# Softmax over partitions by GpSimd all-reduces in place of TensorE, and a scheduled TensorE order, in a two-layer graph kernel

## The chip, the cores and the metric

The kernel runs on one core of a Trainium2 chip. Times are device microseconds of one execution. The kernel before took 2955.12 us, the median of three runs (2951.85 to 2955.24).

The engines are called by their names in the profile: PE (TensorE; PEld its weight loads), DVE (VectorE), ACT (ScalarE), POOL (GpSimd) and SP, which here issues all transfers (SPq is its queue).

## The reference

There are 32 batches of a 512 x 512 matrix x and a 512 x 512 matrix adj, all in float32. Two layers follow each other; each normalizes its input, cuts it at zero and adds its result to the input.

```python
# layer 0
h = relu(layernorm(x))
agg = (adj @ h) / max(rowsum(adj), 1e-6)
x = x + relu(concat([h, agg]) @ W.T)           # W: 512 x 1024
# layer 1
h = relu(layernorm(x))
q, k = split(h @ Wqk);  v = h @ Wv
w = inv_scale * mask * sum(q * (adj @ (k * mask)), -1)
x = x + softmax(w, over the 512 rows)[:, None] * v
```

The softmax runs over the 512 rows of a batch: 512 values of w, which lie as 128 partitions x 4 values. Its maximum and its sum must therefore be taken across partitions.

## The kernel before, in words

**Products.** All large products go through `product` (L121), one level of Strassen's method: seven products of 256 x 256 blocks in place of eight, with sums of blocks made beforehand by `left_sums` and `right_sums` (L103, L112) on DVE. Product k is four matmuls with 128 x 256 results (eight for layer 0's output, which has two terms); the profile shows each as two instructions, so that a product stands there as x8. Its results stand in three PSUM tiles, pp, pr and pq; `keep` (L142) copies some of them to SBUF on ACT (m1, u2, m5, u3; the profile writes m_ and u_ with the product's name), and DVE adds them up. After each product `step()` takes one piece of other work from a list, `background`, so that the other engines' instructions are written between the products.

A batch needs five products: y (layer 0's h by the second half of W, `layer0_y`, L289), o (h by the first half plus adj by y, `layer0_out`, L302), u (adj by the masked h of layer 1, `layer1_u`, L345), t (h of layer 1 by a combined matrix of the two halves of Wqk, multiplied by u and summed, `layer1_t`, L356) and v (`layer1_v`, L376).

**Transposes.** The left operand of a product must stand transposed. The kernel writes a matrix to DRAM scratch and reads it back in another order (`exchange`, L171), then DVE turns 32 x 32 blocks (`to_left`, L179, its instruction in L183). This gives hT (layer 0's h), aT (adj) and h1T (layer 1's h). The scratch transfers are dh and sh for hT, da and sa for aT, d and s for h1T.

**Order.** The main loop (L522 on) runs over i = 0 to 32 and overlaps three batches: u of batch i-1, o of batch i, then t and v of batch i-1, then y of batch i+1. Behind t and v lie, through `background`, the normalization of layer 1 of batch i (`layer1_norm`, L317) and the preparation of hT and aT of batch i+1 (`prepare_h`, L230; `prepare_a`, L256). The pieces of the softmax of batch i-1 and of h1T (`layer1_h`, L334) are taken during y. The loop stands under `tc.manual_schedule` for PE: PE's instructions keep the order in which they are written. On the other engines a scheduler orders the instructions, with the written order as priority; each engine then works through its own queue in that order.

**Normalization.** Statistics of a row block are taken by DVE (`statistics`, L208: L210 and L211); `moments` (L213) turns the variance into 1/sqrt by `pow` on POOL (L216), between two small DVE steps (L215 rstd, L217 nmr); ACT normalizes (`normalize`, L221). For layer 0's h (tile n) the result is written to dh; for layer 1's h (tile h1m) it is written to d, and ACT then scales it by the mask (L327).

**Softmax** (`softmax`, L390). s0: DVE adds up w, multiplies it by the degree and the mask, and takes the maximum of its four values per partition (top, L405). s1: PE transposes top into one row of PSUM (ptop, L409), DVE takes the negative maximum (ntop, L410). s2: PE spreads this one value over the partitions by a matmul with a row of ones (pbc, L414), DVE copies it (nbc, L415), ACT takes the exponential (e, L416), DVE sums four values (es, L417). s3: PE sums over partitions by a matmul with a matrix of ones (psum, L421), DVE takes the reciprocal and scales e (rs, L422; sm, L423). s4: DVE adds sm times v to x (L426), and SP writes x out (L433).

Of the kernel before, what the change touches and what calls it, by code (L numbers as in the profile page):

```python
# [11 lines left out]
AF = mybir.ActivationFunctionType  # L12
ALU = mybir.AluOpType
AX = mybir.AxisListType

P = 128
DEG_EPS = 1e-6
# [4 lines left out]
def kernel(  # L22
# [32 lines left out]
    nc = tc.nc  # L55
# [37 lines left out]
    def drain(n=0):  # L93
        while len(background) > n:
            background.pop(0)()
# [87 lines left out]
        nc.vector.transpose(o, t.rearrange("p k (c r) -> p k c r", r=R))  # L183


    ones = const.tile([P, P], F32, name="ones")
    nc.vector.memset(ones, 1.0)
    mhalf = const.tile([P, C], F32, name="mhalf")
    nc.vector.memset(mhalf, -0.5)

# [8 lines left out]
    def load_x(b):  # L199
        X[b] = load_rows("x", 2, x[b], f"x_{b}")  # L200
# [29 lines left out]
    def prepare_h(b):  # L230

        t = norm_tiles(f"0_{b}")
        d = scratch("dh", f"dh_{b}")
        tiles = {}

        def load():
            n = load_rows("n", 2, x[b], f"n_{b}")
            for c in range(C):
                tiles[c] = n[:, c, :]

        def write(c):
            normalize(tiles[c], tiles[c], t, c)
            nc.sync.dma_start(out=d[c], in_=tiles[c])

        def turn(h):
            if h == 0:
                HT[b] = slots("hT", 1, f"hT_{b}")
            to_left(halves(d), h, HT[b], f"sh_{b}_{h}")

        return (  # L250
            [load] + [lambda c=c: statistics(tiles[c], t, c, f"0_{b}") for c in range(C)] + [lambda: moments(t)]
            + [lambda c=c: write(c) for c in range(C)],
            [lambda: turn(0), lambda: turn(1)],
        )
# [47 lines left out]
    def layer0_out(b):  # L302
        def o(r, cc):
            dst = X[b][:, 2 * r:2 * r + 2, ts(cc, H)]

            def f(p, s):
                if s is not None:
                    t = block("tmp", 5, f"o_{b}_{r}{cc}")
                    add(t, p, s)
                    p = t  # L310
                nc.vector.scalar_tensor_tensor(dst, p, 0.0, dst, op0=ALU.max, op1=ALU.add)

            return f

        product(f"o_{b}", [(HT[b], w1R), (AT[b], Y[b])], o(0, 0), o(0, 1), o(1, 0), o(1, 1))

    def layer1_norm(b):  # L317

        mt = norm_tiles(f"1_{b}")
        t = H1M[b] = slots("h1m", 1, f"h1m_{b}")  # L320
        d = H1T[b] = scratch("d1", f"d1_{b}")

        def one(c):
            v = t[:, 2 * (c // 2):2 * (c // 2) + 2, c % 2, :]
            normalize(v, X[b][:, c, :].rearrange("p (a f) -> p a f", a=2), mt, c)
            nc.sync.dma_start(out=d[c].rearrange("p (a f) -> p a f", a=2), in_=v)
            nc.scalar.activation(v, v, AF.Copy, scale=mraw[:, c, b:b + 1])  # L327

        return (
            [lambda c=c: statistics(X[b][:, c, :], mt, c, f"1_{b}") for c in range(C)] + [lambda: moments(mt)]  # L330
            + [lambda c=c: one(c) for c in range(C)] + right_sums(t)
        )
# [12 lines left out]
    def layer1_u(b):  # L345
        u = U[b] = big.tile([P, 4, 2, H], F32, tag="uv", bufs=1, name=f"u_{b}")

        def o(slot):
            return lambda p, s: add(u[:, slot, :, :], p, s)

        product(
            f"u_{b}", [(AT[b], H1M[b])], o(0), o(1),
            lambda p, _: nc.scalar.activation(u[:, 2, :, :], p, AF.Copy), o(3),
        )
# [35 lines left out]
    def softmax(b):  # L390
        acc = W.pop(b)
        w = small.tile([P, C], F32, tag="w", name=f"w_{b}")
        top = small.tile([P, 1], F32, tag="top", name=f"top_{b}")
        ntop = small.tile([1, 1], F32, tag="ntop", name=f"ntop_{b}")
        nbc = small.tile([P, 1], F32, tag="nbc", name=f"nbc_{b}")
        e = small.tile([P, C], F32, tag="e", name=f"e_{b}")
        es = small.tile([P, 1], F32, tag="es", name=f"es_{b}")
        rs = small.tile([P, 1], F32, tag="rs", name=f"rs_{b}")
        sm = small.tile([P, C], F32, tag="sm", name=f"sm_{b}")

        def s0():
            add(w, acc[:, 0, :], acc[:, 1, :])
            nc.vector.tensor_tensor(w, w, DEG[b], op=ALU.mult)
            nc.vector.tensor_tensor(w, w, mcol[:, :, b], op=ALU.mult)
            nc.vector.tensor_reduce(top, w, AX.X, ALU.max)  # L405

        def s1():
            ptop = ps_s.tile([1, P], F32, tag="s", name=f"ptop_{b}")
            nc.tensor.transpose(ptop, top, identity)  # L409
            nc.vector.tensor_reduce(ntop, ptop, AX.X, ALU.max, negate=True)  # L410

        def s2():
            pbc = ps_s.tile([P, 1], F32, tag="s", name=f"pbc_{b}")
            nc.tensor.matmul(pbc, ones[0:1, :], ntop, start=True, stop=True)  # L414
            nc.vector.tensor_copy(nbc, pbc)  # L415
            nc.scalar.activation(e, w, AF.Exp, bias=nbc)  # L416
            nc.vector.tensor_reduce(es, e, AX.X, ALU.add)  # L417

        def s3():
            psum = ps_s.tile([P, 1], F32, tag="s", name=f"psum_{b}")  # L420
            nc.tensor.matmul(psum, ones, es, start=True, stop=True)  # L421
            nc.vector.reciprocal(rs, psum)  # L422
            nc.vector.tensor_scalar(sm, e, rs, None, op0=ALU.mult)  # L423

        def s4(c):
            nc.vector.scalar_tensor_tensor(  # L426
                X[b][:, c, :], V[b][:, c, :], sm[:, c:c + 1], X[b][:, c, :],
                op0=ALU.mult, op1=ALU.add,
            )
            if c == C - 1:  # L430
                t = X.pop(b)
                for q, dst in enumerate(by_rows(out[b])):
                    nc.sync.dma_start(out=dst, in_=t[q * R:(q + 1) * R, :, :])  # L433

        return [s0, s1, s2, s3], [lambda c=c: s4(c) for c in range(C)]


    w1R, w2R, mR, vR = (slots(n, 1, n, const) for n in ("w1R", "w2R", "mR", "vR"))
# [56 lines left out]
    def weights_late():  # L495
        wqT = big.tile([P, C, 512], F32, tag="uv", bufs=1, name="wqT")
        wkT = slots("h1T", 1, "wkT")[:, 0:4, :, :].rearrange("p s b f -> p (s b f)").rearrange("p (c f) -> p c f", c=C)
        weight_rows(wqk[:, 0:F], wqT, True, "wq")
        weight_rows(wqk[:, F:2 * F], wkT, False, "wk")
        for k in range(2):  # L500
            for dk in range(2):
                p = mm_tile(f"pm_{k}{dk}")
                d = 2 * k + dk
                for a in range(C):
                    nc.tensor.matmul(
                        p.rearrange("p a f -> p (a f)"), wqT[:, a, ts(d, P)], wkT[:, a, :],
                        start=(a == 0), stop=(a == C - 1),
                    )
                nc.scalar.activation(mR[:, 2 * k:2 * k + 2, dk, :], p, AF.Copy)
        for s in right_sums(mR):  # L510
            s()
        tv = load_rows("uv", 1, wv, "tv")
        for c in range(C):
            nc.scalar.activation(
                vR[:, 2 * (c // 2):2 * (c // 2) + 2, c % 2, :],
                tv[:, c, :].rearrange("p (a f) -> p a f", a=2), AF.Copy,
            )
        for s in right_sums(vR):
            s()


    with tc.manual_schedule(engines={mybir.EngineType.PE}):  # L522
        for i in range(B + 1):
            norm = prep = []
            if i > 0:
                layer1_u(i - 1)
                drain()
            if i + 1 < B:
                steps, rest = prepare_h(i + 1)
                background += steps  # L530
            if i < B:
                layer0_out(i)
                drain()
                if i == 0:
                    weights_late()
                norm = layer1_norm(i)
            if i + 1 < B:
                prep = rest + [lambda: left_sums(HT[i + 1])[0](), lambda: left_sums(HT[i + 1])[1]()] + prepare_a(i + 1)
            if i > 0:
                background += norm + prep  # L540
                layer1_t(i - 1)
                layer1_v(i - 1)
                drain()
                first, last = softmax(i - 1)
            else:
                for s in norm + prep:
                    s()
                first = last = []
            background += first + last + (layer1_h(i) if i < B else [])
            if i + 1 < B:  # L550
                layer0_y(i + 1)
            drain()
            if i + 1 < B:
                load_x(i + 1)


# [26 lines left out]
```

## Time and profile before

| what | value |
|---|---|
| median of three runs | 2955.12 us |
| the profiled execution, timed | 2955.12 us |
| its span, first to last instruction | 2953.3 us |
| mean granted PE clock | 0.941 |
| PE busy | 2521.0 us (85%) |
| DVE busy | 1465.5 us (50%) |
| ACT busy | 862.6 us (29%) |
| POOL busy, all but 0.7 us of it the 64 `pow` of L216 | 65.2 us (2%) |
| DMA queue of SP, share of 16 engines | 48.4% |
| one iteration of the loop, steady | 90.45 us |

A line of groups names the line of the code, the engine, the operation, output and input tiles, their shapes and the count; then the busy time in us and the mean of one in ns; then the idle time of the engine just before these instructions and what ended most of it. A chain of waits is followed back from the last instruction: at each step to what released it. A timeline gives start, length, engine, line, tiles and, in brackets, the idle time before and what ended it. Ends of matmuls are modelled, so that neighbouring entries overlap a little.

### The profile page before, as it was taken

How to read it: one execution, taken by the hardware profiler on the slowest of the kernel's cores; microseconds unless marked ns; L12 is line 12 of the kernel's file. 1: busy time of each engine (PE TensorE's matmuls, PEld its weight loads, DVE VectorE, ACT ScalarE, POOL GpSimd, SP SyncE). 2: the span in 40 equal slices, each digit the busy share in tenths (PEclk: the TensorE clock that was granted, in tenths of full speed). 3: DMA queues.
4: the chain of work that ended last, by engine and by line, in shares of the span. 5: the costliest groups of instructions: out<-in, count | busy, mean ns of one | idle time of the engine just before them, and what ended most of it. 6: DMA issues, size and time to landing. Idle time of an engine off the chain costs nothing.

```text
span 2953.3 us, 30565 instructions
## 1 busy us (share of the span) xinstructions
PE 2521.0 (85%) x10948; PEld 2145.5 (73%) x10948; DVE 1465.5 (50%) x3105; ACT 862.6 (29%) x1547; POOL 65.2 (2%) x70
## 2 busy tenths in 40 slices
PE   4798988889988889888898888898888988888988
PEld 3577777777777778777787777787777877777876
DVE  4454544544545545445455455454554544544545
ACT  1332223332233322233222333222332223332232
POOL 0000000000000000000000000000000000000000
PEclk8899999999999999999999999999999999999999
DMA  7554456435465344564454553435634545435342
GB/s 152 131 126 113 114 118 143 111 93 130 96 143 131 93 114 103 129 143 106 91 129 104 143 130 87 123 99 133 143 98 98 126 106 143 121 93 125 90 118 57
DMA packets 363784, 342.91 MB, mean 116 GB/s; under 512 B 27216, under 2 KB 264784, under 8 KB 363632
## 3 DMA queue, kind: packets, MB, share of 16 engines
q1 hardware_dynamic: 363632, 340.96, 48.4%
q8 instruction: 86, 1.41, 0.2%
q14 instruction: 66, 0.54, 0.1%
HBM read 206.64 MB, written 134.22 MB: 115 GB/s over the span
## 4 chain that ended last, share of the span: by engine, by line
PE 66%; DVE 12%; ACT 9%; DMA 6%; SPq 4%; issue 2%; POOL 1%; DVEq 0%; POOLq 0%; ACTq 0%
PE pp_o L131 15%; PE pp_y L131 8%; PE pp_u L131 8%; PE pq_o L131 7%; PE pp_t L131 6%; PE pr_o L131 4%; PE pq_u L131 4%; SPq L176 4%; PE pq_t L131 4%; DVE st L210 4%; ACT h1m L221 3%; DMA n<-in_x_dram 3%; ACT a L276 3%; PE pq_y L131 2%; ACT n L221 2%
## 5 line engine op out<-in xcount | busy, mean ns | idle before, releaser
L131 PE MATMUL pp_y<-w2R,hT 128*128 128x256 f32 x1024 | 298.2, 442 | 244.2 <-DVE hT L183 176.0
L131 PEld LDWEIGHTS pp_y<-w2R,hT 128*128 128x128 f32 x1024 | 219.1, 222 | 300.9 <-issue 201.1
L131 PE MATMUL pq_v<-vR,h1T 128*128 128x256 f32 x512 | 171.9, 495 | 132.3 <-ACT m_v L144 132.3
L131 PE MATMUL pp_v<-vR,h1T 128*128 128x256 f32 x1024 | 257.4, 397 | 1.0 <-ACT m_v L144 1.0
L131 PE MATMUL pp_o<-y,aT 128*128 128x256 f32 x1024 | 245.7, 383 | 12.7 <-DVE aT L183 12.7
L131 PEld LDWEIGHTS pq_v<-vR,h1T 128*128 128x128 f32 x512 | 126.3, 253 | 166.8 <-ACT m_v L144 144.0
L131 PE MATMUL pp_u<-h1m,aT 128*128 128x256 f32 x1024 | 243.2, 381 | 0.0
L131 PE MATMUL pp_t<-mR,h1T 128*128 128x256 f32 x1024 | 241.9, 379 | 0.0
L131 PE MATMUL pp_o<-w1R,hT 128*128 128x256 f32 x1024 | 241.9, 379 | 0.0
L131 PEld LDWEIGHTS pp_v<-vR,h1T 128*128 128x128 f32 x1024 | 207.6, 203 | 35.1 <-ACT m_v L144 1.8
L131 PEld LDWEIGHTS pp_o<-y,aT 128*128 128x128 f32 x1024 | 196.6, 192 | 40.3 <-DVE aT L183 13.2
L131 PEld LDWEIGHTS pp_u<-h1m,aT 128*128 128x128 f32 x1024 | 195.2, 191 | 26.7
L131 PEld LDWEIGHTS pp_t<-mR,h1T 128*128 128x128 f32 x1024 | 194.6, 190 | 26.5
L131 PEld LDWEIGHTS pp_o<-w1R,hT 128*128 128x128 f32 x1024 | 194.6, 190 | 26.5
L98 DVE TENSOR_TENSOR o<-m_o,u_o 128x512 f32<-128x512 f32 x32 | 22.1, 692 | 320.6 <-ACT u_o L144 320.6
L131 PE MATMUL pq_y<-w2R,hT 128*128 128x256 f32 x512 | 128.1, 393 | 4.8 <-DVE hT L98 1.5
L101 DVE TENSOR_TENSOR h1m<-h1m 128x512 f32<-128x512 f32 x128 | 85.3, 687 | 90.2 <-ACT h1m L327 89.2
L216 POOL TENSOR_TENSOR rstd<-rstd,mhalf 128x4 f32<-128x4 f32 x64 | 64.5, 1007 | 2822.4 <-DVE rstd L215 2594.4
L144 ACT ACTIVATE u_o<-pp_o 128x512 f32<-128x512 f32 x64 | 38.2, 597 | 294.3 <-PE pp_o L131 294.3
L131 PE MATMUL pq_o<-y,aT 128*128 128x256 f32 x512 | 121.0, 379 | 0.0
L131 PE MATMUL pq_u<-h1m,aT 128*128 128x256 f32 x512 | 121.0, 379 | 0.0
L131 PE MATMUL pq_t<-mR,h1T 128*128 128x256 f32 x512 | 121.0, 379 | 0.0
(121 smaller groups left out, 3702.6 us busy)
## 6 DMA issues: line engine op xcount, KB each, us to landing
n<-in_x_dram SPq DMA_DIRECT2D x128, 256.0 KB, 6.8
dh<-n SPq DMA_DIRECT2D x128, 256.0 KB, 2.0
a<-in_adj_dram SPq DMA_DIRECT2D x128, 256.0 KB, 9.1
sh<-dh SPq DMA_DIRECT2D x256, 128.0 KB, 3.5
x<-in_x_dram SPq DMA_DIRECT2D x128, 256.0 KB, 6.4
da<-a SPq DMA_DIRECT2D x128, 256.0 KB, 2.2
sa<-da SPq DMA_DIRECT2D x256, 128.0 KB, 3.5
d<-h1m SPq DMA_DIRECT2D x128, 256.0 KB, 2.6
```

What stands on the lines that cost most here:

```text
L98: nc.vector.tensor_tensor(o, a, b, op=ALU.add)
L101: nc.vector.tensor_tensor(o, a, b, op=ALU.subtract)
L131: nc.tensor.matmul(p[:, rc, :], lt[:, LEFT[k], dk, ts(rc, P)], rt[:, RIGHT[k], dk, :], start=first and n == 0, stop=True, skip_group_check ...
L144: nc.scalar.activation(t, p, AF.Copy)
L176: nc.sync.dma_start(out=t[q * R:(q + 1) * R, :, :], in_=src[:, :, ts(q, P)].rearrange("k r j -> r k j"))
L210: nc.vector.bn_stats(st, src)
L216: nc.gpsimd.tensor_tensor(rstd, rstd, mhalf, op=ALU.pow)
L221: nc.scalar.activation(o, i, AF.Relu, scale=t[1][:, c:c + 1], bias=t[2][:, c:c + 1])
L276: nc.scalar.activation(a[c], a[c], AF.Copy, scale=rdeg[:, c:c + 1])
```

## The change

The two matmul steps and the transpose of the softmax are replaced by `partition_all_reduce` on GpSimd, which takes 128 x 1 values and leaves the maximum, or the sum, of all partitions in each partition. `softmax` now has three steps ahead of s4 in place of four. The tile of ones goes. And the main loop no longer stands under `tc.manual_schedule`, so that PE's instructions are ordered by the scheduler like the others'; the body of the loop is otherwise the same, one level less indented.

```diff
+from concourse.bass_isa import ReduceOp as RED
...
-    ones = const.tile([P, P], F32, name="ones")
-    nc.vector.memset(ones, 1.0)
...
-        ntop = small.tile([1, 1], F32, tag="ntop", name=f"ntop_{b}")
+        gtop = small.tile([P, 1], F32, tag="gtop", name=f"gtop_{b}")
+        gs = small.tile([P, 1], F32, tag="gs", name=f"gs_{b}")
...
         def s1():
-            ptop = ps_s.tile([1, P], F32, tag="s", name=f"ptop_{b}")
-            nc.tensor.transpose(ptop, top, identity)
-            nc.vector.tensor_reduce(ntop, ptop, AX.X, ALU.max, negate=True)
-
-        def s2():
-            pbc = ps_s.tile([P, 1], F32, tag="s", name=f"pbc_{b}")
-            nc.tensor.matmul(pbc, ones[0:1, :], ntop, start=True, stop=True)
-            nc.vector.tensor_copy(nbc, pbc)
+            nc.gpsimd.partition_all_reduce(gtop, top, channels=P, reduce_op=RED.max)
+            nc.vector.tensor_scalar(nbc, gtop, -1.0, None, op0=ALU.mult)
             nc.scalar.activation(e, w, AF.Exp, bias=nbc)
             nc.vector.tensor_reduce(es, e, AX.X, ALU.add)
 
-        def s3():
-            psum = ps_s.tile([P, 1], F32, tag="s", name=f"psum_{b}")
-            nc.tensor.matmul(psum, ones, es, start=True, stop=True)
-            nc.vector.reciprocal(rs, psum)
+        def s2():
+            nc.gpsimd.partition_all_reduce(gs, es, channels=P, reduce_op=RED.add)
+            nc.vector.reciprocal(rs, gs)
             nc.vector.tensor_scalar(sm, e, rs, None, op0=ALU.mult)
...
-        return [s0, s1, s2, s3], [lambda c=c: s4(c) for c in range(C)]
+        return [s0, s1, s2], [lambda c=c: s4(c) for c in range(C)]
...
-    with tc.manual_schedule(engines={mybir.EngineType.PE}):
-        for i in range(B + 1):
-            norm = prep = []
...
+    for i in range(B + 1):
+        norm = prep = []
...
```

More of the change, by code (lines that the diff above doesn't have):

```diff
@@ L519, in weights_late @@
             s()
-    with tc.manual_schedule(engines={mybir.EngineType.PE}):
-        for i in range(B + 1):
-            norm = prep = []
[L525 to L551, printed above, removed]
-            drain()
-            if i + 1 < B:
-                load_x(i + 1)
+    for i in range(B + 1):
+        norm = prep = []
+        if i > 0:
+            layer1_u(i - 1)
+            drain()
+        if i + 1 < B:
+            steps, rest = prepare_h(i + 1)
+            background += steps
+        if i < B:
+            layer0_out(i)
+            drain()
+            if i == 0:
+                weights_late()
+            norm = layer1_norm(i)
+        if i + 1 < B:
+            prep = rest + [lambda: left_sums(HT[i + 1])[0](), lambda: left_sums(HT[i + 1])[1]()] + prepare_a(i + 1)
+        if i > 0:
+            background += norm + prep
+            layer1_t(i - 1)
+            layer1_v(i - 1)
+            drain()
+            first, last = softmax(i - 1)
+        else:
+            for s in norm + prep:
+                s()
+            first = last = []
+        background += first + last + (layer1_h(i) if i < B else [])
+        if i + 1 < B:
+            layer0_y(i + 1)
+        drain()
+        if i + 1 < B:
+            load_x(i + 1)
 _INS = ['x', 'adj', 'nodemask', 'L0_gnn_W', 'L1_gnn_Wqk', 'L1_gnn_Wv']
```

## The prediction

> **What bounds the kernel now.** I read the page's busy shares first, then the groups, then one iteration in the chain of waits and in the timeline. The busy shares and two groups:
>
> ```profile
> PE 2521.0 (85%) x10948; PEld 2145.5 (73%) x10948; DVE 1465.5 (50%) x3105; ACT 862.6 (29%) x1547; POOL 65.2 (2%) x70
> ...
> L131 PE MATMUL pp_y<-w2R,hT 128*128 128x256 f32 x1024 | 298.2, 442 | 244.2 <-DVE hT L183 176.0
> ...
> L216 POOL TENSOR_TENSOR rstd<-rstd,mhalf 128x4 f32<-128x4 f32 x64 | 64.5, 1007 | 2822.4 <-DVE rstd L215 2594.4
> ```
>
> TensorE is the bound, but its largest idle time (244 us) lies ahead of one product, y, whose input hT is late. The chain of waits between 1528 and 1573 us shows why (start, length, engine, tile):
>
> ```profile
> 1530.91 2.08 DVE t L366 x12
> 1533.29 1.28 DVE st L210 x2
> 1537.45 1.02 POOL rstd L216
> 1539.41 2.21 ACT n L221 x3
> 1541.62 2.92 ACT h1m L221 x4
> ...
> 1554.13 1.25 DVE hT L183
> 1555.52 3.40 PE pp_y L131 x8
> ```
>
> From the end of t on VectorE (T = 1532.97) a serial path leads to the next y: statistics, `pow` on GpSimd, two normalizations, transfers to DRAM and back, block turns. T to pp_y is 22.55 us here; iterations repeat every 90.45 us and this one stands for them. TensorE's own timeline (start, length, idle before) shows what it does meanwhile:
>
> ```profile
> 1538.65 1.89 PE L131 MATMUL pp_v<-vR,h1T 128*128 128x256 f32 x8
> 1545.07 3.52 PE L131 MATMUL pq_v<-vR,h1T 128*128 128x256 f32 x8 [4.53 <-ACT m_v L144]
> 1548.42 1.89 PE L131 MATMUL pp_v<-vR,h1T 128*128 128x256 f32 x8
> 1555.52 3.40 PE L131 MATMUL pp_y<-w2R,hT 128*128 128x256 f32 x8 [5.20 <-DVE hT L183]
> 1558.75 1.89 PE L131 MATMUL pr_y<-w2R,hT 128*128 128x256 f32 x8
> 1560.48 0.27 PE L409 MATMUL ptop<-identity,top 128*1 128x128 f32 x1
> 1563.02 1.97 PE L131 MATMUL pp_y<-w2R,hT 128*128 128x256 f32 x8 [2.27 <-DVE hT L101]
> 1564.91 0.38 PE L414 MATMUL pbc<-ntop,ones 1*128 1x1 f32 x2
> 1565.22 1.99 PE L131 MATMUL pq_y<-w2R,hT 128*128 128x256 f32 x8
> 1567.05 0.28 PE L421 MATMUL psum<-es,ones 128*128 128x1 f32 x2
> ```
>
> The softmax of before is spread between the seven products of y, after pp_y has begun; it is off the path to y. From pp_y to the first product of u it is 17.32 us for 7 x 1.73 = 12.1 us of work.
>
> [...] eight matmuls of pp_y take 3.40 us after 5.20 us idle, 1.73 warm.
>
> **The change, part by part.** The built program of after shows four things.
>
> (a) Per iteration TensorE loses ptop, pbc and psum (0.27+0.38+0.28 = 0.9 us of the timeline above), and VectorE loses ntop; nbc and rs now read SBUF.
>
> (b) GpSimd gets two all-reduces, and, since they and `pow` are in different libraries, two reloads: one ahead of the maximum, one ahead of `pow`. There are 30 reloads of each kind. Queue: pow n, pow h1m, reload, maximum, sum, reload, pow n. The first reload stands right behind `pow` of the iteration before and waits for nothing: some 80 us hide it. The second stands behind the sum.
>
> (c) The whole softmax up to sm now stands on VectorE's queue directly behind t and **ahead of the statistics**; ScalarE's exponential stands ahead of u2_v. So the path to y gets both all-reduces. Queued behind VectorE's wait: v's sums, all statistics, nmr, and so everything to hT.
>
> (d) TensorE's order is no longer held to the written one: the first product of u goes between the last ones of y, the four normalizations come after all of v's evictions, and n is loaded in one go.
>
> The path to pp_y, from T = 0, with A for an all-reduce (start to end), R for the reload. Hand-overs as measured: 0.17 us DVE to POOL, 0.03 back.
> - w's three steps and top (0.20 pitch, last 0.15): top ends 0.79. Maximum 0.96 to 0.96+A. nbc (0.16), e on ScalarE (0.30), es (0.16) with 0.03 hand-overs: 1.67+A. Sum 1.84+A to 1.84+2A. rs, sm: statistics start at 2.25+2A.
> - The statistics block to rstd is the same six and took 3.99 us (1533.29 to 1537.28): ends 6.24+2A; before 4.31.
> - `pow` can start at 6.41+2A, or when the reload is done: 1.84+2A+R. [...] In general r = R-4.57, not below nothing. [...]
> - nmr 1.04 us later, n on ScalarE 0.20 after that: 7.65+2A+r; before 5.72. The normalization of h1m starts 3.68 after nmr instead of 3.12 (one more sum of v lies between), and ends at E = 14.05+2A+r; before 11.56.
> - From E to hT before: 9.6 us, because the scaling of h1m (L327) stood behind v's eviction, which waited for TensorE's stall. Now scaling follows at once: SP issues sh from E+0.64, the fourth at E+2.2 to E+2.7, landing 3.5 us later, and the sums of h1m end about E+5.4. I take E+6.2, and pp_y at E+7.6 = 21.65+2A+r.
> So pp_y moves by -0.90+2A+r.
>
> From pp_y to the end of u's first product: 3.40+1.73 for the first two; then VectorE adds y (0.67) and hT (0.67) and TensorE waits 1.57 instead of 2.27; with u as filler the rest runs without softmax matmuls to 17.1 us. Before it took 17.32+1.73 = 19.05. **That gives back 1.95.** The rest of the iteration (u, o, t) has no idle time before and gets none: aT is ordered some 2 us earlier against pp_y. TensorE's idle in v vanishes, but v isn't on the path; what is late next is only hT.
>
> Sum per iteration: D = 2A + r - 2.85.
>
> **The unknown A.** Low end: the cheapest comparable GpSimd row, the affine select of 128x128, 0.29 us. [...] `pow` itself takes 1.01 us without crossing partitions, so I take half more: A = 1.5. **R:** low end 0.1 us (the reload [...] at the start of before, leaves 0.08 us between two instructions), [...]
>
> D = 3.0+1.38-2.85 = 1.53; 30 iterations have this path (y of batches 2 to 31): +46 us. At the edges I take 6 us off: at the end v's sums wait for the softmax no more (ptop to sm, 2.6 us, runs beside v, and two of four outputs go early), and at the start two products of o fill a wait for aT. Profiled span 2953.3+46-6 = 2993.3. Outside the span lie 1.8 us (2955.12 timed), and the profiled run equals the median of the runs, so the prediction is **2995 us**, +1.3%.
>
> **Rivals.**
> - **The all-reduces are cheap, faster than before.** Speaks for: one value per partition. A = 0.3 gives D = 0.6+1.38-2.85 = -0.87, x30 = -26, -6: 2923 us. It decides from 2A+r = 2.85 downwards, in the stretch from top to `pow`. Chance 0.20.
> - **The all-reduce is slow.** A = 4: D = 8+1.38-2.85 = 6.53, +196-6: 3145 us. ScalarE's e then also holds back u2_v, but TensorE's idle only moves within v. Chance 0.18.
> - **The load is paid at the first call, not at the reload,** so nothing hides it: [...] 3310 us. Chance 0.12.
> - **Nothing measurable:** A about 0.75, within 6 us of before. Chance 0.08.
> - The forecast: 0.42.
>
> That the change doesn't do what it says is excluded: the built program has the instructions. Under about 0.2% a measurement of this kernel can't tell a difference from no change. Slower: 0.42+0.18+0.12 = 0.72; same 0.08; faster 0.20. Cases of both signs hold the chance; the forecast alone, with A from 1 to 2.2 and 0.5 us of error in the 2.85, spans 2960 to 3040. The range leaves out the late load and the outer half of the cheap case, where the reload costs nothing too: 2905 to 3165.
>
> **What would show it.** In the profile of after: two all-reduces per batch on POOL (A); pow of n 7 to 8 us + 2A behind the end of t (r); one long idle ahead of pp_y of about 14 us where there were two of 5; no idle ahead of pq_v; the wait of y for hT's sums below 2.3; u between y. Wrong would be: idle elsewhere (aT, h1m), a scaling of h1m that still comes late, or a gap ahead of the maximum.

## The result, and the profile after

The changed kernel takes 2972.60 us (median of four runs, 2969.87 to 2980.39) against 2954.55 us before (median of four, 2951.85 to 2955.24): ratio 1.0067, 95% interval 1.0047 to 1.0087. It is slower, by 18 us; the forecast was 40. Its profiled execution is the fastest of the four, 2969.87 us, span 2968.1 us, so that the two profiled spans lie 14.8 us apart. The page's busy shares, and the group of y:

```profile
PE 2431.5 (82%) x10788; PEld 2094.1 (71%) x10788; DVE 1467.5 (49%) x3072; ACT 878.1 (30%) x1547; POOL 101.4 (3%) x134
...
L132 PE MATMUL pp_y<-w2R,hT 128*128 128x256 f32 x1024 | 299.5, 444 | 431.8 <-DVE hT L184 431.5
```

PE is busy for 90 us less (30 us of small softmax matmuls are gone, and the groups pp_v and pq_v take 64 us less) and waits longer: ahead of pp_y stand 432 us of idle time in 31 waits, where before had 176 (31 waits), 132 in v and 68 for hT's sums. POOL's groups, from the groups view:

```profile
L215 POOL TENSOR_TENSOR rstd<-rstd,mhalf 128x4 f32<-128x4 f32 x64 | 76.0, 1187 | 524.8 <-DVE rstd L214 307.6 <-issue 192.0 <-ACT n L220 18.4
L414 POOL PARTITION_ALL_REDUCE gs<-es x32 | 12.6, 393 | 32.7 <-DVE es L411 32.7
L408 POOL PARTITION_ALL_REDUCE gtop<-top x32 | 12.2, 380 | 2281.6 <-DVE top L405 2269.8 <-issue 6.0 <-DVE h1m L102 5.8
```

An all-reduce takes 0.38 to 0.39 us. The reloads have no line of their own: where the built program has one and the next input is there, the trace shows "issue", idle time that nothing else explains. Before, with `pow` alone, has none of it ahead of its 64 `pow`; e12 below, with all-reduces alone, none ahead of its 64 all-reduces. In the changed kernel 192 us of it stand ahead of `pow` in 27 waits, 6.0 ahead of the maximum in one, and the 5.8 us under "DVE h1m" are one more, in the last batch but one. Such a wait is counted from the end of the instruction before, so that it also holds the time in which the input was not there yet. One iteration of POOL's timeline (start, length, line, tiles, idle before), with T, the end of t on DVE, at 1454.43:

```profile
1455.35 0.38 POOL L408 PARTITION_ALL_REDUCE gtop<-top  x1 [77.58 <-DVE top L405]
1456.55 0.39 POOL L414 PARTITION_ALL_REDUCE gs<-es  x1 [0.81 <-DVE es L411]
1463.89 1.05 POOL L215 TENSOR_TENSOR rstd<-rstd,mhalf 128x4 f32<-128x4 f32 x1 [6.95 <-issue]
1467.32 1.35 POOL L215 TENSOR_TENSOR rstd<-rstd,mhalf 128x4 f32<-128x4 f32 x1 [2.37 <-DVE rstd L214]
```

`pow` of n starts 6.95 us after the sum, although its input was ready at 1461.81, 2.1 us ahead of it (2.2 on average over 27 iterations). The first reload is hidden in the 77.58 us. The chain of waits of the same iteration (start, length, piece) does not go through POOL at all:

```profile
1463.72 1.74 PE pp_v L132 x8
...
1465.49 0.02 ACT v L386
...
1466.01 2.88 ACT n L220 x4
...
1468.90 2.94 ACT h1m L220 x4
...
1474.17 3.41 DMA sh<-dh
```

It comes from PE's last product of v: ACT evicts it (L386) and only then normalizes n, although nmr of n is ready at 1465.14; h1m follows without a gap, then the transfers and hT. PE's timeline shows the one long wait, eight matmuls behind it in 3.53 us instead of 1.73, and the short wait for hT's sums:

```profile
1463.56 1.89 PE L132 MATMUL pp_v<-vR,h1T 128*128 128x256 f32 x8
1479.10 3.53 PE L132 MATMUL pp_y<-w2R,hT 128*128 128x256 f32 x8 [13.65 <-DVE hT L184]
...
1485.90 1.53 PE L132 MATMUL pq_y<-w2R,hT 128*128 128x256 f32 x6 [1.54 <-DVE hT L99]
```

Times from T, from the timelines of 27 iterations (n and h1m: medians; the others: means). The runs below stand in the same table, e7 and e8 apart, where n starts ahead of T; their labels are shortened to the number.

| run | time, us | ratio to before (95%) | n starts | h1m done | pp_y starts | pp_y to next T | period |
|---|---|---|---|---|---|---|---|
| before | 2954.6 | | 5.71 | 11.56 | 23.26 | 67.24 | 90.50 |
| changed | 2972.6 | 1.0067 (1.0047-1.0087) | 11.55 | 17.52 | 24.85 | 65.82 | 90.66 |
| e1 free PE order alone | 2994.5 | 1.0137 (1.0122-1.0152) | 11.55 | 17.28 | 25.38 | 66.06 | 91.44 |
| e5 GpSimd softmax alone | 3025.2 | 1.0244 (1.0227-1.0261) | 11.79 | 17.54 | 25.04 | 67.76 | 92.80 |
| e2 no reload | 3005.7 | 1.0176 (1.0159-1.0193) | 11.98 | 18.96 | 26.30 | 65.87 | 92.17 |
| e9 n ahead of v's eviction | 2972.2 | 1.0062 (1.0047-1.0077) | 10.81 | 17.51 | 24.89 | 65.89 | 90.78 |
| e10 both | 2906.3 | 0.9836 (0.9822-0.9851) | 7.54 | 15.11 | 22.44 | 66.31 | 88.75 |
| e3 softmax late | 3014.1 | 1.0206 (1.0191-1.0221) | 11.55 | 17.29 | 26.19 | 65.97 | 92.15 |
| e4 softmax late, n first | 3009.1 | 1.0188 (1.0173-1.0203) | 8.54 | 14.72 | 26.01 | 66.17 | 92.18 |
| e6 before, logarithm | 2901.6 | 0.9825 (0.9810-0.9840) | 4.46 | 11.45 | 21.59 | 67.16 | 88.75 |
| e11 all-reduces in the old order | 2939.5 | 0.9949 (0.9932-0.9966) | 5.38 | 11.24 | 22.35 | 67.67 | 90.03 |
| e12 the same, logarithm | 2899.1 | 0.9814 (0.9799-0.9829) | 4.05 | 11.05 | 21.27 | 67.47 | 88.74 |
| e13 the same, free PE order | 2950.3 | 0.9990 (0.9983-0.9996) | 4.06 | 11.42 | 18.77 | 71.67 | 90.44 |

So in steady state the change costs only 0.16 us an iteration (+1.59 ahead of pp_y, -1.42 behind it). Most of the 14.8 us between the two spans, 10.3 us, is already there at T of the third softmax (355.92 before, 366.19 after). Two things stand out there. At the first maximum the reload is not hidden, since `pow` of h1m has only just ended. And in the second iteration `pow` of n starts at T+12.83, where later ones start near T+9.6; POOL's timeline, and the DVE instruction just ahead of the statistics:

```profile
188.02 1.01 POOL L215 TENSOR_TENSOR rstd<-rstd,mhalf 128x4 f32<-128x4 f32 x1 [1.86 <-ACT n L220]
194.98 0.38 POOL L408 PARTITION_ALL_REDUCE gtop<-top  x1 [5.96 <-issue]
...
280.49 0.69 DVE L99 TENSOR_TENSOR v<-m_v,u_v 128x512 f32<-128x512 f32 x1 [3.53 <-ACT u_v L145]
...
285.26 1.06 POOL L215 TENSOR_TENSOR rstd<-rstd,mhalf 128x4 f32<-128x4 f32 x1 [8.77 <-DVE rstd L214]
```

In the second iteration the reload is hidden: `pow` waits for its input, whose statistics stand on DVE behind a sum of v, which waits 3.53 us for ACT. And the exposed reload of the first is not shown to be what costs the time. From the first T to the third the kernel before takes 168.0 us and the changed one 178.0, but e1 below, which has no reload, takes 177.1, nearly as long, and e2, without the reload ahead of `pow`, 176.2; e5, with both reloads and PE's order held, takes 173.7. How the loss at the start divides between the order and the reload stays open.

### The profile page after: what moved, and what is told of

Read it like the earlier page. It is cut to its first block, busy times and chain, and to the rows that moved or that the text cites. A ratio compares the mean times of both kernels' runs of the same rounds, so it can differ in the third digit from the quotient of the medians.

```text
span 2968.1 us, 30448 instructions
## 1 busy us (share of the span) xinstructions
PE 2431.5 (82%) x10788; PEld 2094.1 (71%) x10788; DVE 1467.5 (49%) x3072; ACT 878.1 (30%) x1547; POOL 101.4 (3%) x134
## 3 DMA queue, kind: packets, MB, share of 16 engines
q8 instruction: 85, 1.39, 0.2%
## 4 chain that ended last, share of the span: by engine, by line
PE 79%; DVE 5%; ACT 5%; DMA 4%; SPq 2%; issue 2%; POOL 2%; DVEq 0%; ACTq 0%; POOLq 0%
PE pp_o L132 15%; PE pp_y L132 10%; PE pp_u L132 7%; PE pp_t L132 7%; PE pq_o L132 7%; PE pp_v L132 6%; PE pq_y L132 4%; PE pq_u L132 4%; PE pq_t L132 4%; PE pr_o L132 4%; DMA sh<-dh 3%; ACT h1m L220 3%; PE pq_v L132 3%; PE pr_y L132 2%; PE pr_t L132 2%
## 5 line engine op out<-in xcount | busy, mean ns | idle before, releaser
L132 PE MATMUL pp_v<-vR,h1T 128*128 128x256 f32 x1024 | 244.0, 381 | 6.9 <-ACT m_v L145 5.5
L132 PEld LDWEIGHTS pp_v<-vR,h1T 128*128 128x128 f32 x1024 | 195.4, 191 | 34.8 <-ACT m_v L145 5.9
L99 DVE TENSOR_TENSOR o<-m_o,u_o 128x512 f32<-128x512 f32 x32 | 22.1, 692 | 265.3 <-ACT u_o L145 265.3
L132 PEld LDWEIGHTS pq_y<-w2R,hT 128*128 128x128 f32 x512 | 94.6, 189 | 72.7 <-issue 59.1
L132 PE MATMUL pq_o<-w1R,hT 128*128 128x256 f32 x512 | 121.1, 379 | 0.1
L132 PE MATMUL pq_v<-vR,h1T 128*128 128x256 f32 x512 | 120.9, 379 | 0.0
```

Source lines behind the costliest of these rows:

```text
L99: nc.vector.tensor_tensor(o, a, b, op=ALU.add)
L132: nc.tensor.matmul(p[:, rc, :], lt[:, LEFT[k], dk, ts(rc, P)], rt[:, RIGHT[k], dk, :], start=first and n == 0, stop=True, skip_group_check ...
```

## Experiments

Two theories of why n, and with it y, comes late. Theory A: the reload ahead of `pow` holds up n and with it hT. Theory B: ACT's order does, which puts v's last eviction ahead of n.

**e1, the free order alone.** The kernel before with the loop's `with tc.manual_schedule(...)` removed.

> The kernel before with one part of the change alone: TensorE's order is no longer held to the written one; softmax, ones and pow stay as before, so GpSimd has no switch of library. Theory A (the switch of GpSimd's library ahead of pow costs the time): nothing of that is here, n is normalized from T+5.7 as before and pp_y begins near T+21.7 (T is the end of t on VectorE); with the 1.4 us that y gains, the period falls by about 2.9 us and the time is about 2870 us. Theory B (the order on ScalarE costs it: the changed schedule puts v's last eviction ahead of the normalization of n, so n waits for TensorE's last product of v): n starts near T+11.1 without any reload, pp_y near T+24.3, and the time lies between 2945 and 2970 us, close to before.

Measured: 2994.5 us, 40 more than before: theory B's start of n, and worse than either theory's time. ACT's timeline:

```profile
1473.36 0.60 ACT L387 ACTIVATE v<-pp_v 128x512 f32<-128x512 f32 x1 [2.86 <-PE pp_v L131]
1473.86 2.92 ACT L221 ACTIVATE n<-n,nmr,rstd 128x512 f32<-128x512 f32 x4
```

nmr is ready at 1470.76 (T+8.45), and n still waits until T+11.55 for v, with no reload in the kernel. DVE's queue changed too: the first sum of v now stands ahead of the statistics and waits 1.71 us for pr_v, so `pow` starts at T+7.25 where before had 4.5. PE has psum ahead of pp_y (5.84 us of waiting for es), and DVE's softmax stands ahead of h1m's sums and hT.

**e5, GpSimd's softmax alone.** The changed kernel with the loop under `manual_schedule` for PE again.

> The other part of the change alone: softmax's maximum and sum on GpSimd, with TensorE held to the written order as before. ScalarE still has v's last eviction ahead of n, and VectorE the softmax ahead of the statistics. If the order on ScalarE and VectorE is what counts: n again near T+11.5, pp_y near T+24.9, and without u's first matmuls between those of y the period is 0.5 to 1.5 us longer than in the changed kernel: 2985 to 3010 us. If the free order of TensorE itself had cost the time: 2930 to 2955 us.

Measured: 3025.2 us, above the expected range; n and pp_y as expected, 1.94 us more behind pp_y than in the changed kernel. The halves cost 40 and 72 us, the whole 18: they do not add up, since each half also reorders ACT and DVE.

**e2, no reload.**

```diff
+    leps = const.tile([P, 1], F32, name="leps")
+    nc.vector.memset(leps, LN_EPS)
+    nc.scalar.preload_act_table_set("natural_log_exp_and_others")
...
-        nc.vector.tensor_scalar(rstd, mv[:, :, 1], LN_EPS, None, op0=ALU.add)
-        nc.gpsimd.tensor_tensor(rstd, rstd, mhalf, op=ALU.pow)
+        nc.scalar.activation(rstd, mv[:, :, 1], AF.Ln, bias=leps)
+        nc.scalar.activation(rstd, rstd, AF.Exp, scale=-0.5)
```

> The changed kernel, with rstd as exp(-0.5 ln(var + eps)) on ScalarE in place of pow on GpSimd, so GpSimd has nothing but the all-reduces and no switch of library after the first; softmax still ahead of the statistics. Theory A (reload): nmr is ready near T+8, n starts there and not at T+11.56, the period falls by 2 to 3 us: about 2885 to 2910 us. Theory B (order on ScalarE): the logarithm and n stand behind u3_v and v, n starts near T+12, half a microsecond later than in the changed kernel, only the exposed first load of 6 us at the start is saved: 2970 to 2985 us.

Measured: 3005.7 us. Theory A is wrong as a sole cause: without any reload n starts at T+11.98. Theory B has n right; the time is 20 us above its range, because h1m's logarithm stands behind n's normalizations and h1m is done 1.44 us later.

**e9, only ACT's order.** v's last eviction is queued behind n.

```diff
-        out21(pp, None)
+        with behind("last"):
+            out21(pp, None)
...
+            lambda w: tc.issue_after(LAST[b + 2].ins) if w in ('last',) and b + 2 in LAST else nullcontext(),
```

Here LAST[b] is the last normalization of n; in the trace the eviction lands behind h1m's normalizations too. 

> The changed kernel, only v's last eviction queued behind n and h1m on ScalarE; the reload stays. If two chains end together ahead of h1m (the reload through pow, nmr and VectorE's queue; v's eviction through ScalarE's), then taking one away alone gives little: n 0.8 us earlier (near T+10.8, when nmr is ready), h1m near T+14.5 as before, 2965 to 2980 us. If the order on ScalarE alone were the cause: n from T+8, pp_y 2.5 us earlier, 2890 to 2905 us.

Measured: 2972.2 us, no change. Theory B is wrong as a sole cause. ACT's timeline (T = 1453.16):

```profile
1464.49 2.93 ACT L222 ACTIVATE n<-n,nmr,rstd 128x512 f32<-128x512 f32 x4 [3.13 <-DVE nmr L218]
1468.27 2.92 ACT L222 ACTIVATE h1m<-x,nmr,rstd 128x512 f32<-128x512 f32 x4 [0.85 <-DVE nmr L218]
```

n is earlier and waits for nmr (the reload). h1m waits for its own nmr: the rest of its statistics stands on DVE behind nmr of n, and so the reload's delay reaches h1m too.

**e10, both.** e2's edit, and u3_v as well as v's last eviction behind n.

> Both chains taken away at once: rstd by logarithm and exponential on ScalarE (no reload), and u3_v and v's last eviction queued behind n; softmax still ahead of the statistics on VectorE. If the two chains hold h1m together: n near T+8.2, h1m normalized near T+15.5, pp_y near T+22.1 against 24.86: about 2.7 us per iteration, 2880 to 2905 us, where each alone gave nothing. If the softmax ahead of the statistics is what costs, wherever it is: 2950 us or more.

Measured: 2906.3 us, just past the expected 2905; pp_y at T+22.44 against the expected 22.1. The softmax is still ahead of the statistics. Together the edits take 66 us off the changed kernel; e2's alone added 33 and e9's gave 0. **Two chains end together ahead of h1m**: in the changed kernel's iteration above, nmr of h1m ends at 1468.87 and n at 1468.90. What each chain is worth is less clear. e10 also moves u3_v, which e9 did not, and e2's edit takes away not the reload alone: it also shortens the way to rstd, which gave 52 us in e6 below, where there is no reload at all. So the order on ACT is shown to cost 99 us where no reload hides it (e2 against e10), but the reload's own price is not separated from that of `pow`.

**e3 and e4, the softmax behind the statistics.** s0's first step queued on DVE behind nmr of h1m; e4 with u3_v and v's last eviction behind n as well.

```diff
-            add(w, acc[:, 0, :], acc[:, 1, :])
+            with tc.issue_after(NMR[b + 1].ins) if b + 1 in NMR else nullcontext():
+                add(w, acc[:, 0, :], acc[:, 1, :])
```

> The changed kernel with the whole softmax queued behind the statistics of n and of h1m on VectorE, so that both reloads stand behind pow and are hidden; ScalarE's order is left as it falls out (v's evictions ahead of n). Theory A (reload and all-reduces on the path): all of that is off the path, nmr is ready near T+5.6, pp_y near T+19, about 2830 to 2870 us. Theory B (order on ScalarE): n still waits for v's last eviction, now some 0.5 us earlier since the exponential no longer holds u2_v back: n near T+10.6 to 11.1, the period 0.5 to 1 us shorter than in the changed kernel and the start some 6 us: 2940 to 2955 us.

> The same, and on ScalarE u3_v and v's last eviction queued behind the four normalizations of n. Theories A and B agree here: n starts near T+5.7 and h1m is normalized by T+11.6; pp_y near T+19.5 to 21 unless h1m's scaling behind v's eviction comes late again; the period falls by 4 to 5 us: 2815 to 2855 us. Theory B says that nearly all of the gain comes with this edit, theory A that it was there with the softmax late.

Measured: 3014.1 and 3009.1 us; both expectations missed, and by the same oversight. POOL's timeline of e4:

```profile
1575.25 1.01 POOL L218 TENSOR_TENSOR rstd<-rstd,mhalf 128x4 f32<-128x4 f32 x1 [2.24 <-DVE rstd L217]
1582.39 0.38 POOL L416 PARTITION_ALL_REDUCE gtop<-top  x1 [6.13 <-issue]
```

The reload ahead of the maximum had some 77 us to hide in; put right behind `pow` it costs most of its 6.13 us: the maximum starts 5.27 us after its input, top, has ended (1577.12). DVE waits for the maximum with h1m's sums and hT behind it, so pp_y starts at T+26.0 although h1m was done 2.8 us earlier.

**e7 and e8, an order written out.** e4's edit of ACT; on DVE the statistics of n ahead of v's sums, hT ahead of h1m's sums, the softmax behind both (all by `issue_after`); e8 the same in the kernel before with PE free.

> The changed kernel with four places in the queues fixed: on VectorE the statistics of n ahead of v's sums, hT's turns and sums ahead of h1m's sums, and the softmax behind both; on ScalarE u3_v and v's last eviction behind n. Both reloads then stand where nothing waits for them. If the order is what the change loses by: pp_y 4 to 6 us earlier than in the changed kernel, until v's late evictions bound TensorE: 2790 to 2880 us, faster than both kernels. If the reloads or the all-reduces cost something wherever they stand: 2940 us or more.

> The same four places fixed in the kernel before, TensorE's order left free, softmax still by TensorE. With the softmax off the path in both, the difference to the run before this one is what GpSimd's maximum and sum are worth by themselves: 0.9 us of small matmuls per iteration less on TensorE, and no wait of TensorE for VectorE's softmax steps: 0 to 1.5 us per iteration, so this one is 0 to 45 us slower than the other, 2800 to 2920 us.

Measured: 2993.7 (ratio 1.0136, 1.0121 to 1.0152) and 3010.4 us (1.0193, 1.0178 to 1.0208): both far slower than expected. pp_y's own wait fell to 0.30 us, but PE now waits for h1T's sums within t (3.63 us), for ACT in v (5.29) and for hT's sums (2.82), in sum 12.7 us as against 12.0 before. Moving the statistics forward also put them ahead of t's last steps. Why h1T comes late I did not follow. e7 is faster than e8 by 17 us, within the expected 0 to 45.

**e6, e11, e12: the exchange with the old order put back.** e6 is the kernel before with e2's edit. e11 is the changed kernel with PE under `manual_schedule`, the softmax behind hT's sums on DVE, and n ahead of u3_v and v's last eviction; e12 adds e2's edit.

> Control for the run without a reload: the kernel before with rstd by logarithm and exponential on ScalarE in place of pow on GpSimd, nothing else. ScalarE keeps n ahead of v's evictions here, so the shorter step counts: n 0.5 to 0.8 us earlier, pp_y with it if h1m's scaling does not wait for v instead: 2930 to 2950 us. If the form with the logarithm itself is slow (its time on ScalarE, more evictions late): 2955 to 2985 us.

> The all-reduces alone in the kernel before: TensorE held to the written order, n ahead of the late evictions of v, statistics directly behind t, and the softmax behind hT's sums on VectorE as before; pow stays on GpSimd, so both reloads are there (one behind pow of h1m, one behind the sum), some 60 us ahead of whoever needs them. If an all-reduce costs 0.4 us and a reload nothing where it is hidden: 2935 to 2955 us, level with before or a little faster by the three small matmuls. If a reload or an all-reduce slows others wherever it stands: 2970 us or more.

> The same with the logarithm in place of pow, so no reload: the order of the run before_ln (2901.6 us) with GpSimd's maximum and sum in place of TensorE's. If the exchange itself is worth 0 to 0.9 us per iteration: 2875 to 2903 us, the fastest so far. If hidden reloads had a price, it is this run's lead over the previous one beyond the 52 us that the logarithm gave without all-reduces.

Measured: 2901.6, 2939.5 and 2899.1 us. e6 is 28 us better than expected; e11 and e12 lie in their ranges. POOL's timeline of e11:

```profile
1532.94 1.01 POOL L218 TENSOR_TENSOR rstd<-rstd,mhalf 128x4 f32<-128x4 f32 x1 [1.92 <-ACT n L223]
1557.28 0.38 POOL L413 PARTITION_ALL_REDUCE gtop<-top  x1 [23.33 <-DVE top L410]
1558.47 0.39 POOL L419 PARTITION_ALL_REDUCE gs<-es  x1 [0.81 <-DVE es L416]
1618.87 1.06 POOL L218 TENSOR_TENSOR rstd<-rstd,mhalf 128x4 f32<-128x4 f32 x1 [60.00 <-DVE rstd L217]
```

Both reloads lie in gaps that end with the real producer, not with "issue". Hidden, they and the all-reduces cost little or nothing: e11 is 14 us faster than before. But its gain lies ahead of pp_y (22.35 against 23.26), and the softmax stands behind it, so the order is not quite that of before; behind pp_y e11 takes 0.43 us an iteration more, and e12 0.31 more than e6. Between e6 and e12 the exchange is worth nothing that can be told (their intervals overlap). These two are the fastest of all and beat both kernels; what they gain comes with the logarithm, not with GpSimd. Shorter steps alone do not account for it: in e6 h1m is done only 0.1 us earlier than before, pp_y 1.7. ACT's queue has changed too: u_v and m_v now stand ahead of h1m's normalization, and PE's wait in v is 2.3 us where before had 4.5:

```profile
1511.50 3.59 PE L131 MATMUL pp_v<-vR,h1T 128*128 128x256 f32 x8 [2.27 <-ACT u_v L144]
```

How the 52 us divide between the two was not tried.

**e13, e12 with PE's order free,** and v's sums on DVE behind nmr of n, to keep the statistics first.

> As the run before (all-reduces at the softmax's old place, no reload, n ahead of v's late evictions, statistics ahead of v's sums; 2899.1 us), with TensorE's order free, so that u's first product fills the waits of y: what the free order is worth where none of the queues is spoilt by it. If it is worth what the changed kernel shows between pp_y and the end of t (1.44 us per iteration): 2850 to 2865 us, and the changed kernel's loss lies wholly ahead of pp_y. If the free order gives nothing by itself, or pushes t back behind v's matmuls: 2890 to 2910 us.

Measured: 2950.3 us, slower than expected either way, by the mechanism that its expectation names last: measured from T, pp_y starts 2.5 us earlier than in e12, but T itself is late. The last product of t now stands behind two and a half products of v (20 of their matmuls, 2.5 x 1.73 = 4.3 us), and pp_y to the next T grows from 67.47 to 71.67. PE's timeline:

```profile
1437.24 1.46 PE L132 MATMUL pp_v<-vR,h1T 128*128 128x256 f32 x6
1438.53 1.89 PE L132 MATMUL pr_v<-vR,h1T 128*128 128x256 f32 x8
1440.26 1.03 PE L132 MATMUL pq_v<-vR,h1T 128*128 128x256 f32 x4
1441.12 1.89 PE L132 MATMUL pp_t<-mR,h1T 128*128 128x256 f32 x8
```

## Why the prediction was right and wrong

The steps that failed are terms of its sum: "2A", taken as 3.0 us an iteration, measured 0.77, and the edges, taken as -6 us, measured about +10. Between them stand three smaller errors.

- **Direction: right, but in good part by luck.** The loss is ahead of pp_y and the gain behind it, as forecast, and the two nearly cancel: 27 iterations of the steady state lose 4.5 us, where 46 were forecast for 30. Most of what was measured is lost in the first two iterations, where the prediction had a small gain.
- **The place: right.** One idle of 13.65 us in place of two, no idle in v, the wait for hT's sums 1.54 (predicted 1.57), u between y; E to pp_y took 7.3 (predicted 7.6). The path to n was not the predicted one: with the measured A and R it gives n at T+10.95 (7.65 + 0.77 + 2.53), and n starts at T+11.55, behind v's last eviction.
- **A, mis-sized.** I took 1.5, half more than `pow`; measured 0.385. "2A" is 0.77 in place of 3.0: -2.23 us an iteration.
- **R and r, mis-sized.** My r of 1.38 rests on a length of the reload that no trace of before shows. The first exposed one ahead of the maximum took 5.96 us, which would give 1.39. But the reload back to `pow` shows as 6.7 to 7.6 us in the steady state, 7.10 on average from the sum's end. With R = 7.10, r = 2.53 in place of 1.38: +1.15. This error hid part of the one in A. The low end, 0.08 us ahead of the affine select at the start of before, was no bound: at the same place the changed kernel shows 8.99 us of "issue", up to 9.92.
- **The base, mis-chosen.** I took 22.55 from one iteration; before alternates between that and 23.9, mean 23.26. That makes the step 0.7 too large.
- **What is given back:** 1.95 predicted, 1.42 measured. e5 against the changed kernel gives 1.94 for PE's free order with GpSimd's softmax in both; before, with the softmax on PE, was 0.5 better than e5.
- With these four, D = 1.53 - 2.23 + 1.15 - 0.7 + 0.5 = 0.25, against 0.16 measured; over 30 iterations 5 to 8 us instead of 46.
- **The edges failed.** "At the edges I take 6 us off": measured +10.3 at the start and about nothing at the end, where 3.1 us are lost in the last two iterations and as much is gained behind the last T. I had read that the first reload is hidden by 80 us, which does not hold for the first iteration, nor for the last but one. But e1, without any reload, is 9.9 us behind at the third T too (365.84), so the start cannot be put down to the reload. What e1 shares with the changed kernel is the free order of PE, which the prediction had priced at the start only as a gain (two products of o that fill a wait for aT).
- **"A second chain" was missing.** I wrote that the four normalizations come after v's evictions, and priced it at nothing. e1 shows that the free order moves n by 5.8 us without a reload: nmr is 2.8 us later, behind DVE's other order, and n another 3.1 behind that, behind ACT's. In the changed kernel this chain hides behind the reload, and the reload behind it (e2, e9, e10). So the sum above comes out right with the reload alone, but whoever took the reload away on its strength would have gained nothing.
- **The rivals.** Cheap all-reduces (A = 0.3, 2923 us) had A right and still missed by 50 us, for R, the base, the gain and the start. "Nothing measurable" was nearest for the steady state, and it too left out the start. The slow all-reduce and the load at the first call are excluded by 0.38 us and by the hidden first reload.

## What to carry over

A switch of GpSimd's library has no line in these views of the profile; here it showed as 5.84 to 7.63 us of idle time ahead of the next instruction, as "issue" or, twice in the changed kernel, under the name of another. It did not show where the next input came later anyway (gaps of 8.8 to 78 us in the changed kernel), and did where the input was ready first. Look at the first iteration, and at every place to which the step is moved, for that cover. Where two in-order queues lead to the same instruction, take both waits away in one run before calling either harmless: here each alone gave nothing or a loss, and both, with a shorter way to rstd among them, gave 2.2%. Before a loss is put down to a cost that is visible in the trace, look for a run without that cost: at the start of this kernel e1 lost nearly as much without any reload. Freeing PE's order reordered the others' queues too (in e1 n moved from T+5.71 to T+11.55), so read those queues ahead of pricing it.

## What the runs showed of the hardware

- An all-reduce of 128x1 in float32 over 128 partitions takes 0.38 us (maximum) and 0.39 us (sum) on average in the changed kernel, 0.35 and 0.38 in e12 and e13; single ones in e3, e7, e9 and e11 took 0.38 and 0.39.
- The two directions of the switch differ: ahead of the maximum, where it is exposed, 5.96 and 5.84 us in the changed kernel (the maxima at 194.98 and 2910.67), 6.19 in e3 (at 1584.93) and 6.13 in e4 (the line shown above); back to `pow` 6.7 to 7.6 us in the changed kernel. The `pow` of h1m took 1.35 us in the steady state of the changed kernel and 1.01 us in e1, e4 and e11; why was not tried.
- An idle time of PE was not followed by the same speed each time. After 2.27 us in v in e6 (the line shown above) the next eight matmuls took 3.59 us, after 1.86 us in v in e12 (at 1510.17) 3.28 us; after 2.75 us in y in e12 (at 1532.16) they took 1.97 us, and so did those of before after 2.27 us in y (at 1563.02). Without a wait such a line reads 1.89 us. In before the granted clock was 0.57 over the 3.40 us of pp_y that follow 5.20 us of idle time (from 1555.52), and 1.00 in the 1.6 us from 1558.80. So 1.86 us of idle time was once followed by a line 1.4 us longer and 2.75 us by one 0.1 us longer; what decides was not tried.
- Two ACT steps of 128x4 (logarithm 0.29 us, exponential 0.20, means of e12) replace `pow` of 1.01 and its hand-overs. With one table set named at the start, the trace of e12 holds one table load in all, 1.28 us, as before and the changed kernel do.
